# Three small moves in a graph network with expert layers: gate spread, one residual sum, first tile's norm

## The chip, the cores and the metric

The kernel runs on one core of a Trainium2 chip. Its time is the time on the device in microseconds (us), median of a few runs. Five engines work side by side, each through its own list in order: TensorE (PE in the profile, its weight loads PEld), VectorE (DVE), ScalarE (ACT), GpSimd (POOL) and SyncE (SP), which here issues the loads. They wait for each other by semaphores.

## The reference

The reference takes 625 nodes with 768 features and a list of edges and computes eight layers, always a graph layer and then an expert layer, each on the normed x and added to it (a residual). What matters here:

- Layer 0, graph attention with 12 heads of 64 features: for each head a softmax over a node's neighbours weights the neighbours' features; `out = relu(agg + res)`, where `res` is a linear map of the input. The 12 x 64 outputs side by side are added to x.
- Expert layers 0, 1 and 3: a router gives each node eight logits, the two best experts get weights from a softmax, and the output is the weighted sum of `gelu(toks @ w1e) @ w2e` over the chosen experts. An expert has 192 hidden features. In layer 1 the experts have biases, and an attention over all nodes stands before them.
- Layers 1 and 2 (graph convolutions), expert layer 2 (soft slots) and layer 3's graph attention are not touched by the change. Layer 3's graph attention needs, for every head, the products of its weights with two attention vectors; these depend on weights alone.

## The kernel before, in words

x is kept in SBUF as five tiles of 125 nodes. Instructions are written in one stream; a planner then orders them for each engine by its own estimates of time, and it may take an instruction ahead of one written before it. Tiles come from pools with a fixed number of places; in PSUM there are four places of 1024 floats, given out in the order written (`ps()`), so a new one waits until an old one has been read.

*End of layer 0* (`L0_gnn`, lines 780 to 914). For each head `gather` multiplies weights and features on PE, ACT copies the result (`gat_o`, L835), and `back` turns it back to nodes by five transposes (L848), divides by the softmax's sum and adds it to `res` on DVE (L851, L853). Two heads are one group of 128 features. After head 9 a loop (L896 to L902) takes groups 0 to 4: for groups 3 and 4 a relu on ACT (`positive`, L864), for all a sum of x and `res` on POOL (L900), then the statistics of the new x on DVE (`stats`, L868). The last head's `back` runs in two parts, tiles 0 to 3 and tile 4, and calls `last` for each tile, which adds the last group to x (L872), takes its statistics and calls `final`. `final` norms a tile (`ln_tile`, L181 to L191: mean and variance, square root on ACT, reciprocal, scaling) and turns the tile before it with `turn_due`: six transposes on PE (L198) and a copy to `xT` by ACT (L202). Both parts of the last head's `back` write one PSUM tile.

*Expert layers* (`experts`, from L962). The hidden layer has 12 blocks of 128 features, taken in pairs. A pair's products are made by a scheme of seven products of half size (`half_begin`, `half_rest`): `first` makes products 1 and 2, `rest` makes 6, 7, 5, 4 and 3, all through the helper at L136, with sums of the weights made by POOL beforehand (`sums`, L338 to L342) and sums of the results on DVE (L412, with `U2` the running one). Between the sixth and the seventh product of the first pair `choose` takes the router's logits, turns them (L260) and works out the gates on DVE (`gates`, L917 to L960). Behind the first pair, five matmuls for `gT3` (L1025) turn the gates and split them in three bf16 parts; `gate` then spreads them over 128 rows with PE (L129) and multiplies the hidden block on DVE (L1009). In expert layer 1 five more transposes (L1033) give the gates for a bias.

*Down-product* (`down`, from L1048). The first tile is multiplied as it is (60 matmuls with the first product of the next); L1080 adds it to x, and `final(0)` norms it. Then the weights' sums (`right_sums`, L444 to L447) and, for tiles 1 and 2 and then 3 and 4, seven products with sums on DVE (L1116) and one copy by ACT (L1124). The steps of layer 3's attention vectors are done beside it where there is time (`vectors`, called as `beside`): each loads 128 rows of weights through SP (L1287) into one of two places and makes two dots with them on DVE (L1298); a copy (L1297) holds them behind the work given as the second argument. In expert layers 0 and 1 seven steps are done in the down-product:

```
            prod(4, b2, (t + 1, 0))
            if t == 1:
                sums(3)
                if beside:
                    beside(7, U3[:, 0:1])
```

Of the kernel before, what the change touches and what calls it, by code (L numbers as in the profile page):

```python
# [14 lines left out]
ALU = mybir.AluOpType  # L15
# [3 lines left out]
P = 125  # L19
NT = N // P  # L20
# [3 lines left out]
NEXP = 8  # L24
# [11 lines left out]
class Net:  # L36
# [559 lines left out]
    def L0_gnn(self):  # L596
        nc, tc, a, x = self.nc, self.tc, self.a, self.x
# [4 lines left out]
        with ExitStack() as ctx:  # L602
# [236 lines left out]
            def back(h, then=None):  # L839

                o = outs[h]
                p = self.ps()[:P, 0 : NT * 128].rearrange("p (t c) -> p t c", c=128)
                rden = self.small.tile([P, NT, 1], F32, tag="rden", name="rden")
                hs = slice(h * DH, (h + 1) * DH)
                for part in (range(4), range(4, NT)) if then else (range(NT),):
                    a, b = part[0], part[-1] + 1
                    for t in part:
                        nc.tensor.transpose(  # L848
                            p[:, t, 0 : DH + 1], o[:, TILES[t]], self.ident[: DH + 1, : DH + 1]
                        )  # L850
                    nc.vector.reciprocal(rden[:, a:b], p[:, a:b, DH : DH + 1])  # L851
                    for t in part:
                        nc.vector.scalar_tensor_tensor(  # L853
                            res[:, t, hs], p[:, t, 0:DH], rden[:, t], res[:, t, hs],
                            ALU.mult, ALU.add,
                        )
                        if then:
                            then(t)
                if h % 2 and h < H - 5:
                    positive(h // 2)  # L860

            def positive(g):
                hs = slice(g * 128, (g + 1) * 128)
                nc.scalar.activation(res[:, :, hs], res[:, :, hs], AF.Relu)  # L864
# [15 lines left out]
            for i in range(H + 4):  # L880
                if i < H:
                    ms[i], us[i] = self.gat_largest(tmpp, mb, a1[i], a2[i])
                if 0 <= i - 2 < H:
                    h = i - 2
                    self.gat_exp(
                        ws[h], a1[h], us[h], a1s[:, 0, :, h], pieces=1 if i < H else NT
                    )
                steps = [(back, i - 4), (gather, i - 3)]
                for f, h in steps if i < H else reversed(steps):
                    if 0 <= h < H - (f == back):  # L890
                        f(h)
                if i < H:
                    score(i)
                if i == H + 1:

                    for g in range(H // 2 - 1):  # L896
                        if g >= H // 2 - 3:
                            positive(g)
                        hs = slice(g * 128, (g + 1) * 128)
                        nc.gpsimd.tensor_tensor(x[:, :, hs], x[:, :, hs], res[:, :, hs], ALU.add)  # L900
                        for t in range(NT):
                            stats(t, g)  # L902
            back(H - 1, then=last)
# [58 lines left out]
    def experts(self, over_all, w1, w2, gelu, b1=None, b2=None, after=None, beside=None):  # L962

        nc, tc, a, x = self.nc, self.tc, self.a, self.x
        with tc.tile_pool(name="moe", bufs=1) as big, ExitStack() as up_pool:
            bc = self.column(b1, NF) if b1 else None
            if b2:
                b2t = big.tile([NEXP, D], F32, name="b2t")
                nc.sync.dma_start(b2t, a[b2])
            hg = big.tile([128, NF, N], F32, name="hg")  # L970
            gT3 = big.tile([3 * NEXP, N], BF16, name="gT3")
            gT = big.tile([NEXP, N], F32, name="gT") if b2 else None
            sel = self.sel.rearrange("p e f -> p (e f)")
            ws = [self.weight(a[w1][:, g * 512 : (g + 1) * 512], KD, 512) for g in range(3)]
            upp = up_pool.enter_context(tc.tile_pool(name="moeup", bufs=1))
            late, prods, begun = [], {}, {}
            B = self.half_nodes(upp, late=late)


            def sums(c):  # L980
                prods[c] = self.half_products(upp, B, ws[c // 4], *(
                    slice((c % 4 + o) * 128, (c % 4 + o + 1) * 128) for o in range(2)
                ))

            def first(c):

                w, js = ws[c // 4], slice(c % 4 * 128, (c % 4 + 1) * 128)
                begun[c] = self.half_begin(
                    upp, [(w[:, ks, js], b) for ks, b in zip((slice(0, 3), slice(3, 6)), B)],
                    hg[:, c, :],  # L990
                )

            def rest(c, between=None):
                if c + 2 < NF:
                    sums(c + 2)
                self.half_rest(
                    prods.pop(c), begun.pop(c), hg[:, c, :], hg[:, c + 1, :], between
                )
                for o in range(2):
                    h = self.n3(hg[:, c + o, :])  # L1000
                    nc.scalar.activation(
                        h, h, gelu, bias=bc[:, c + o : c + o + 1] if b1 else 0.0
                    )

            def gate(c):
                gv = self.nv(self.ps(), 128)
                self.mm_nodes(gv, [sel[:, c * 128 : (c + 1) * 128]], [self.n3(gT3)])
                h = self.n3(hg[:, c, :])
                nc.vector.tensor_tensor(h, h, gv, ALU.mult)  # L1009

            sums(0)
            for c in (0, 2, 4):
                first(c)
            self.turn_due(NT - 1)
            late[0]()
            turned, gb = self.logits(big), []

            def choose():
                turned()
                gb.append(self.gates(over_all))  # L1020

            rest(0, choose)
            pv = self.nv(self.ps(), 3 * NEXP)
            for t in range(NT):
                nc.tensor.matmul(  # L1025
                    pv[:, t, :], gb[0][:, t].rearrange("p e i -> p (e i)"), self.identb[:P, :P],
                    start=True, stop=True,
                )
            nc.vector.tensor_copy(self.n3(gT3), pv)
            if b2:  # L1030
                pv = self.nv(self.ps(), NEXP)
                for t in range(NT):
                    nc.tensor.transpose(pv[:, t, :], self.lg[:, t, :], self.ident[:P, :P])  # L1033
                nc.vector.tensor_copy(self.n3(gT), pv)
            for c in range(2, NF + 2, 2):
                if c < NF:
                    if c not in begun:
                        first(c)
                    rest(c)
                for o in (c - 2, c - 1):  # L1040
                    gate(o)
                if beside and c < NF:
                    beside(1, hg[:P, c + 1, 0:1])
            up_pool.close()
            with tc.tile_pool(name="moedown", bufs=1) as dp:
                self.down(dp, a[w2], hg, gT, b2t if b2 else None, after, beside)

    def down(self, pool, w2, hg, gT, b2t, after, beside):  # L1048
# [29 lines left out]
            self.mm(p[:, 512 * j : 512 * j + HD], lhs, rhs)  # L1078
        xv = halves(x[:, 0, :])
        nc.vector.tensor_tensor(xv, xv, self.hv(p, P), ALU.add)  # L1080
        if after:
            self.final(0)
        else:
            for j in range(2):
                store(0, j)

# [13 lines left out]
        for t in (1, 3):  # L1100
# [4 lines left out]
            def prod(n, to, bias=None):  # L1105
                A, B = pr[n - 1]
                lhs = [A[:, c, :] for c in range(HB)]
                rhs = [B[:, c, :] for c in range(HB)]
                if b2t is not None and bias:
                    g, j = bias  # L1110
                    lhs.append(db[:, t // 2] if g is None else gT[:, TILES[g]])
                    rhs.append(b2t[:, j * HD : (j + 1) * HD])
                self.mm(to, lhs, rhs)

            def add(out, in0, in1=None):
                nc.vector.tensor_tensor(out, out if in1 is None else in0, in0 if in1 is None else in1, ALU.add)  # L1116
# [8 lines left out]
            add(x11, U2)  # L1125
            prod(6, a2)
            add(U2, U2, a2)
            prod(7, b1)
            add(U3, U2, b1)
            add(x12, U2)  # L1130
            prod(4, b2, (t + 1, 0))
            if t == 1:
                sums(3)
                if beside:
                    beside(7, U3[:, 0:1])
            if after:
                self.turn_due(t - 1)
            add(x21, U3)
# [17 lines left out]
                continue  # L1156
            for o in (t, t + 1):
                self.final(o, hold=True)

    def experts_beside(self, *args, **kw):  # L1160

# [1141 lines left out]
```

## Time and profile before

| what | us |
|---|---|
| median of 3 runs (1931.92 to 1932.81) | 1932.52 |
| the profiled execution | 1933.47 |
| its span | 1931.8 |
| PE busy (8314 matmuls) | 1855.9 |
| DVE, POOL, ACT busy | 1134.9, 601.8, 526.2 |
| layer 0, about 0 to 231: PE busy | 186.0 |
| expert layer 0, about 231 to 392: PE busy | 154.4 of 161 |
| attention of layer 1, about 475 to 718: PE busy | 238.2 of 243 |
| expert layer 1, about 718 to 892: PE busy | 168.0 of 174 |
| expert layer 3, about 1779 to 1932: PE busy | 144.9 of 153 |

Up to about 140 us DVE, ACT and POOL share the chain with PE; behind that PE is nearly always busy, and the chain that ended last is PE for 83% of the span. In lines of the timeline the first number is the start, the second the length; then engine, line, operation, output and inputs, shapes, and how many instructions are merged; in brackets how long the engine stood idle before, and for whom. The granted clock (PEclk) is a share of full speed. Busy time of PE contains slow matmuls too, so the clock has to be read with it.

### The profile page before, as it was taken

To read this page: it belongs to the slowest core of one execution; us is meant where nothing else is said; L and a number is where in the kernel's file an instruction comes from. 1 tells how busy PE (TensorE), PEld (TensorE's weight loads), DVE (VectorE), ACT (ScalarE), POOL (GpSimd) and SP (SyncE) were. 2 spreads that over 40 slices of the span, in tenths; PEclk is the share of its full clock that TensorE was granted. 3 is DMA by queue.
4 is the path that set the end of the run, shared out by engine and by line. 5 is a ranking of instruction groups with operands and counts; after the bars stand their busy time and mean duration, and the time that the engine had idled before them with its cause. 6 is when DMAs were issued, how large, how long until landed. Compare 5 with 4: busy or idle time off the path is not lost.

```text
span 1931.8 us, 21712 instructions
## 1 busy us (share of the span) xinstructions
PE 1855.9 (96%) x8314; PEld 1274.8 (66%) x8314; DVE 1134.9 (59%) x2226; ACT 526.2 (27%) x961; POOL 601.8 (31%) x515
## 2 busy tenths in 40 slices
PE   7968899999999999999999999999999999999999
PEld 6844565555677766655556778878667888556665
DVE  8789857647566756674835464554546555145562
ACT  2379611002254532100111131322314233111200
POOL 1079624234410052343015222231035321402331
PEclk9969899999999999999999999999999999999999
DMA  2040112120300022213510211000011121020111
GB/s 68 21 142 37 36 37 66 53 80 12 103 26 25 1 96 90 71 52 115 156 65 31 76 36 63 26 25 33 1 43 35 39 71 65 1 98 25 47 35 32
DMA packets 64021, 103.16 MB, mean 53 GB/s; under 512 B 7301, under 2 KB 37223, under 8 KB 63918
## 3 DMA queue, kind: packets, MB, share of 16 engines
q1 hardware_dynamic: 63658, 101.69, 16.2%
q8 instruction: 66, 1.08, 0.2%
q14 instruction: 37, 0.30, 0.1%
q10 hardware_dynamic: 260, 0.09, 0.0%
HBM read 99.81 MB, written 1.95 MB: 53 GB/s over the span
## 4 chain that ended last, share of the span: by engine, by line
PE 83%; DVE 7%; POOL 4%; ACT 2%; issue 1%; DMA 1%; SPq 1%; ACTq 0%; DVEq 0%; POOLq 0%
PE ps L136 65%; PE ps L129 3%; POOL gat_w L560 2%; PE ps L777 2%; PE ps L1806 2%; PE ps L1461 2%; PE ps L1493 2%; PE ps L1480 1%; PE ps L198 1%; PE ps L1675 1%; PE ps L143 1%; DMA av_w<-in_L_gnn_W 1%; PE ps L715 1%; DVE gat_w L591 1%; ACT gat_w L593 1%
## 5 line engine op out<-in xcount | busy, mean ns | idle before, releaser
L338 POOL TENSOR_TENSOR S<-w 128x384 f32<-128x384 f32 x40 | 41.5, 1042 | 453.6 <-PE ps L136 354.8
L136 PE MATMUL ps<-xT,w 128*128 128x313 f32 x480 | 137.9, 431 | 0.7 <-ACT pr L1469 0.7
L136 PE MATMUL ps<-w,xT 128*125 128x384 f32 (+2 forms) x392 | 125.3, 473 | 0.0
L136 PE MATMUL ps<-T,w 128*128 128x313 f32 x408 | 121.5, 428 | 0.0
L560 POOL TENSOR_TENSOR gat_w<-gat_w,xT 125x625 f32<-125x625 f32 x60 | 86.3, 1469 | 101.0 <-DVE xT L532 94.0
L136 PEld LDWEIGHTS ps<-xT,w 128*128 128x128 f32 x480 | 89.1, 190 | 35.1 <-issue 2.7
L136 PE MATMUL ps<-T,S 128*128 128x313 f32 x348 | 107.5, 444 | 1.8 <-DVE T L318 1.4
L136 PEld LDWEIGHTS ps<-w,xT 128*125 128x125 f32 x392 | 72.8, 188 | 46.6 <-issue 11.7
L136 PE MATMUL ps<-w,S 128*125 128x384 f32 x292 | 100.2, 488 | 2.8 <-DVE x L1116 2.8
L136 PE MATMUL ps<-xT,S 128*128 128x313 f32 x336 | 102.7, 433 | 0.0
L136 PE MATMUL ps<-w,hg 128*125 128x384 f32 x288 | 96.5, 488 | 0.9 <-DVE hg L1009 0.9
L136 PEld LDWEIGHTS ps<-T,w 128*128 128x128 f32 x408 | 76.0, 189 | 29.9 <-DVE U L358 1.4
L136 PE MATMUL ps<-hh,gat_w 125*125 125x257 f32 (+1 forms) x400 | 89.8, 379 | 0.0
L136 PEld LDWEIGHTS ps<-T,S 128*128 128x128 f32 x348 | 65.6, 195 | 30.7 <-issue 5.1
L136 PE MATMUL ps<-w,x2T 128*125 128x384 f32 (+1 forms) x280 | 84.1, 449 | 0.0
L136 PEld LDWEIGHTS ps<-w,S 128*125 128x125 f32 x292 | 54.3, 188 | 43.9 <-DVE x L1116 4.0
L136 PEld LDWEIGHTS ps<-hh,gat_w 125*125 125x125 f32 x400 | 73.3, 187 | 11.3 <-issue 0.4
L136 PEld LDWEIGHTS ps<-w,hg 128*125 128x125 f32 x288 | 53.1, 188 | 39.9 <-issue 2.2
L777 PE MATMUL ps<-ohd,ohs 125*125 125x313 bf16 x425 | 66.4, 312 | 12.2 <-DVE ohs L770 12.2
L136 PEld LDWEIGHTS ps<-xT,S 128*128 128x128 f32 x336 | 61.0, 189 | 25.0 <-issue 4.1
L1298 DVE CUSTOM_DVE_ANT_0 av_junk<-av_w,av_a 128x512 f32<-128x512 f32 (+1 forms) x80 | 72.2, 902 | 8.9 <-DMA av_w<-in_L_gnn_W 7.2
L569 DVE CUSTOM_DVE_ANT_0 junk<-ps,mb 125x625 f32<-125x625 f32 x85 | 68.5, 806 | 13.5 <-PE ps L143 8.7
(442 smaller groups left out, 3795.9 us busy)
## 6 DMA issues: line engine op xcount, KB each, us to landing
w<-in_L_ffn_phiT SPq DMA_DIRECT2D x8, 1536.0 KB
w<-in_L_gnn_W SPq DMA_DIRECT2D x8, 1536.0 KB
w<-in_L_ffn_w SPq DMA_DIRECT2D x6, 1152.0 KB
w<-in_L_gnn_W SPq DMA_DIRECT2D x6, 1152.0 KB
av_w<-in_L_gnn_W SPq DMA_DIRECT2D x24, 256.0 KB
av_w<-in_L_gnn_W SPq DMA_DIRECT2D x16, 384.0 KB
w<-in_L_ffn_w SPq DMA_DIRECT2D x3, 1536.0 KB
w<-in_L_ffn_qkv_wT SPq DMA_DIRECT2D x6, 768.0 KB
```

Source lines behind the costliest of these rows:

```text
L129: self.nc.tensor.matmul(pv[:, s, :], lhs[i], rhs[i][:, s, :], start=i == 0, stop=i == n - 1)
L136: self.nc.tensor.matmul(out, lhs[i], rhs[i], start=i == 0, stop=i == n - 1)
L143: self.nc.tensor.transpose(pv[:, t, :], col(t).to_broadcast([P, rows]), self.ident[:P, :P])
L198: nc.tensor.transpose(pv[:, k, :P], src[:, k * 128 : (k + 1) * 128], self.ident[:P, :P])
L338: nc.gpsimd.tensor_tensor(S1, A21, A22, ALU.add)
L560: nc.gpsimd.tensor_tensor(w[:, s, :], w[:, s, :], lc[:, s, :], ALU.add)
L569: nc.vector.tensor_tensor_reduce(self.n3(junk), row, self.n3(mb[:, t, :]), 1.0, -3e38, ALU.subtract, ALU.max, m[:, t : t + 1],)
L777: nc.tensor.matmul(acc[j // 2][:, j % 2, :], ohs[:, TILES[j]], ohd[:, 0:HN], start=c == cs[0], stop=c == cs[-1],)
L1298: nc.vector.tensor_tensor_reduce(junk, wt, row, 1.0, 0.0, ALU.mult, ALU.add, dst)
L1461: nc.tensor.matmul(sv[r][:, s, :], qk[half[r], 0, TILES[t]], self.n3(qk[half[r], 1, :])[:, s, :], start=True, stop=True,)
L1493: nc.tensor.matmul(ov[half[r]], v[:, s, h * DH : (h + 1) * DH], pT[r][:, s, :], start=s == 0, stop=s == NT - 1,)
L1806: nc.tensor.matmul(pv[:, j, :], zTs[t][:, k, :], w2[k // 3][:, k % 3, js], start=k == 0, stop=False,)
```

## The change

1. In `back`, the second part of the last head's transposes writes a PSUM tile of its own.
2. In the loop behind head 9, group 4 (heads 8 and 9) no longer goes through a relu on ACT and a sum on POOL: one DVE step makes `max(res, 0) + x`. Group 3 stays as it was.
3. In the expert layers, the matmuls that turn the gates, and the copies of their results, become the function `chosen`, which is called between the sixth and the seventh product of the second pair (blocks 2 and 3, the third and fourth of the twelve blocks) instead of ahead of that pair.
4. In the down-product of layers with a next stage (expert layers 0 and 1), `final(0)` is called behind the sixth product of the first two tiles instead of behind the first tile, and the seven steps of attention vectors behind these tiles' norms instead of behind their fourth product.

```
@@ back @@
                     a, b = part[0], part[-1] + 1
+                    if a:
+                        p = self.ps()[:P, 0 : NT * 128].rearrange("p (t c) -> p t c", c=128)
                     for t in part:
@@ L0_gnn, the loop behind head 9 @@
                     for g in range(H // 2 - 1):
-                        if g >= H // 2 - 3:
-                            positive(g)
                         hs = slice(g * 128, (g + 1) * 128)
-                        nc.gpsimd.tensor_tensor(x[:, :, hs], x[:, :, hs], res[:, :, hs], ALU.add)
+                        if g == H // 2 - 2:
+                            nc.vector.scalar_tensor_tensor(
+                                x[:, :, hs], res[:, :, hs], 0.0, x[:, :, hs], ALU.max, ALU.add
+                            )
+                        else:
+                            if g == H // 2 - 3:
+                                positive(g)
+                            nc.gpsimd.tensor_tensor(
+                                x[:, :, hs], x[:, :, hs], res[:, :, hs], ALU.add
+                            )
                         for t in range(NT):
                             stats(t, g)
@@ experts @@
+            def chosen():
+                pv = self.nv(self.ps(), 3 * NEXP)
+                for t in range(NT):
+                    nc.tensor.matmul(
+                        pv[:, t, :], gb[0][:, t].rearrange("p e i -> p (e i)"),
+                        self.identb[:P, :P], start=True, stop=True,
+                    )
+                nc.vector.tensor_copy(self.n3(gT3), pv)
+                if b2:
...
             rest(0, choose)
-            pv = self.nv(self.ps(), 3 * NEXP)
...
             for c in range(2, NF + 2, 2):
                 if c < NF:
                     if c not in begun:
                         first(c)
-                    rest(c)
+                    rest(c, chosen if c == 2 else None)
@@ down @@
         nc.vector.tensor_tensor(xv, xv, self.hv(p, P), ALU.add)
-        if after:
-            self.final(0)
-        else:
+        if not after:
             for j in range(2):
                 store(0, j)
...
             prod(6, a2)
             add(U2, U2, a2)
+            if after and t == 1:
+                self.final(0)
             prod(7, b1)
...
             if t == 1:
                 sums(3)
-                if beside:
-                    beside(7, U3[:, 0:1])
...
             for o in (t, t + 1):
                 self.final(o, hold=True)
+            if beside and t == 1:
+                beside(7, U3[:, 0:1])
```

More of the change, by code (lines that the diff above doesn't have):

```diff
@@ L1020, in choose @@
                 gb.append(self.gates(over_all))
-            rest(0, choose)
-            pv = self.nv(self.ps(), 3 * NEXP)
[L1024 to L1034, printed above, removed]
+            def chosen():
[7 more added lines that the diff above has]
+                if b2:
+                    pv = self.nv(self.ps(), NEXP)
+                    for t in range(NT):
+                        nc.tensor.transpose(pv[:, t, :], self.lg[:, t, :], self.ident[:P, :P])
+                    nc.vector.tensor_copy(self.n3(gT), pv)
+            rest(0, choose)
             for c in range(2, NF + 2, 2):
```

## The prediction

> **What bounds the kernel now.** I read the page's slices first, then the waits of the matmul engine (PE) from 225 us on, then the chain in order of time around each wait, then the granted clock in short windows, and last the timeline of those places.
>
> ```profile
> PE   7968899999999999999999999999999999999999
> PE ps L1025 <- DVE gb L959: 7.8, 3, 2.6
> PE ps L848 <- DVE lt_r L183: 4.3, 1, 4.3
> PE ps L136 <- DVE x L1116: 2.8, 2, 1.6
> PE ps L136 <- ACT U L1124: 1.8, 2, 1.2
> ```
>
> After the first eighth of the span PE is busy in nine tenths or more of every slice, so time is won only where PE stands still or runs slowly. The waits (total, number, longest) name the few places. The change touches the first three: the spread of the gates (L1025, once in each of three expert layers), the last head of the first layer (L848), and the down-product (L1116).
>
> ```profile
> 258.97 0.45 PE ps L1025 x5
> 259.42 6.63 PE ps L136 x18
> ...
> 1801.06 4.95 PE ps L136 x18
> ```
>
> ```profile
> 258.00:260.00 2.00, 1.03 (x7) 0.88 0.00 0
> 260.00:262.00 2.00, 2.00 (x6) 0.50 0.00 0
> 262.00:264.00 2.00, 2.00 (x7) 0.77 0.00 0
> 752.00:754.00 2.00, 2.00 (x5) 0.50 0.00 0
> 1800.00:1802.00 2.00, 1.38 (x9) 1.00 0.03 8
> ```
>
> The same 18 matmuls after the gate spread take 6.63 us in the first layer and 4.95 in the last. The windows (stretch, length, PE busy, then the granted clock) say why: after the 2.6 us stall PE runs at half clock in the first two layers, not in the last. In tenths of a microsecond the half clock lasts from 259.51 to 262.92 and from 751.03 to 754.44, 3.41 us each, and costs half of that, 1.7 us.
>
> ```profile
> 222.18 1.06 DVE L868 BATCH_NORM_STATS2 st<-x 125x6 f32<-125x128 f32 x5 [2.04 <-POOL x L900]
> 224.34 0.17 DVE L851 RECIPROCAL rden<-ps 125x4 f32<-125x4 f32 x1
> 226.67 0.44 PE L848 MATMUL ps<-ident,gat_o 65*125 65x65 f32 x1 [4.28 <-DVE lt_r L183]
> 231.48 2.89 PE L198 MATMUL ps<-ident,xn 125*128 125x125 f32 x12 [1.04 <-DVE xn L191]
> 850.70 0.55 DVE L1116 TENSOR_TENSOR x<-x,ps 125x384 f32<-125x384 f32 x1
> 851.30 4.13 PE L136 MATMUL ps<-w,S 128*125 128x384 f32 x12 [1.61 <-DVE x L1116]
> ```
>
> At the end of the first layer VectorE (DVE) stands 2.04 us for POOL's last sum; the last head's division starts at 224.34 although its transposes were done at 222.40, and PE turns the last two tiles from 231.48. In the fourth layer's down-product PE stands 1.61 us for one DVE sum.
>
> **End of the first layer.** Removed: ScalarE's relu (219.82, 0.72) and POOL's sum (220.62, 1.53); added: one DVE step of 125x640 right after the statistics that end at 218.43. Its price: 0.75 to 0.80 by the L1009 row (128x625 at 1.51 for two), so about 219.2. The reciprocal of dinv waits for ScalarE until 219.9 in any case; the statistics then run 220.1 to 221.2, head 10's transposes end at 221.48, its division takes 0.18 + 1.05, and the last head's starts at 222.7 instead of 224.34: -1.6. The new PSUM tile moves the fifth tile's transposes behind the turns of tiles 0 to 2 on PE (+0.44 between two turns), and its five DVE steps (228.05 to 229.70) behind tile 2's norm, which is no longer queued after them; ScalarE now takes both square roots ahead of its copies. Stepping through: tile 0 turned from 225.9, tile 1 to 228.85, tile 2 to 230.3, the odd transposes to 230.75, tile 3 (ScalarE's norm ends 230.9) to 232.3, against 234.37. I take -2.0. Bounds: DVE beside POOL can be three times slower (L1116: 1.69 beside POOL's L466, 0.55 alone), so the new step beside POOL's five AT sums might take 2.4; that and a half clock that lasts to 235.6 as now leave -0.2. If the shorter idle (222.40 to 225.9) escapes the half clock, turns take 0.80 as at 244.37 instead of 1.45, and it is -3.4. The fifth tile's norm ends near 233.5; it is turned at 242.5, so it is covered. SP issues nothing here, and POOL's next sums (L338, from 230.00) may start 1.5 us later, when the layer's memory comes free; the first pair's end near 237 and are asked for at 245.6.
>
> [...]
>
> **Gates.** Nothing is added; five small matmuls per layer move behind the third pair's first product, 6 matmuls of 1.58 us (1792.05 to 1793.63 from start to start). Its sums by POOL were made 10 us and more before (in the first expert layer by 239.9), and its PSUM slot is the logits', long read. So it fills 1.6 of each 2.6 us gap and leaves 1.0: three times -1.6, or -4.8. Gaps of 1.0 to 1.6 us elsewhere (738, 850) show a clock of 1.00, so the half clock in two layers goes too: -1.7 (6.63 against 4.95) and -1.7: -3.4. Against it: the planner now puts the four gate products behind the fourth product, where they used to cover DVE's sums between two products. Here the three last products of the pair cover: DVE's sum after the seventh product (0.2 + 0.48) lies beside 1.1 us of the fifth. In the next pair the first attention dot (1.05 beside POOL at 272.37) is queued ahead of the U sum that PE's seventh product needs: by my steps the sum is done 10.0 to 10.6 us after the gate spread, PE asks at 10.4. I charge 0.3 for two layers (0 to 2 as bounds; the last layer has no dots). From 259 to 315 PE and its weight loads, released by PE, make the chain, so the gain reaches the end. Sum -7.9.
>
> **Down-product.** The call for the first tile's norm is written later, but in the planned order of DVE, ScalarE and PE it stands where it stood, right behind the weights' sums and ahead of ScalarE's U copy: nothing. What moves is the seven steps of attention vectors: the copy L1297 and fourteen dots now follow two sums of x, and SP's order of their loads is the same. In the fourth layer one dot that waits for its load (849.95) falls behind the sum that PE waits for: that sum can run at about 848.9, and PE's next product is ready at 849.69, so -1.6. The first dots start 0.45 later, which costs 0 to 0.45 in the second layer, where the load-paced dots stay ahead of that sum (stall 1.15). I take -1.3, bounds 0 and -1.6.
>
> **Sum.** -2.0 - 7.9 - 1.3 = -11.2 on the profiled execution's 1933.47 is 1922.3. The median of the three runs is 0.95 below that execution, where a half clock more or less could lie; subtracted from it the sum gives 1921.3. I say 1922.0. All bounds together: -13.2 from the median (1919.3) to -3.0 from the profiled time (gates -4.8 + 2, first layer -0.2, down 0; 1930.5).
>
> **Rivals.**
> - *The half clock is luck (0.12).* The two drops lie 491.52 us apart, 144 times 3.413: fixed windows. A 2.6 us gap lowers the clock only when enough of it falls in one; in the last layer it did not. If the timed runs mostly missed, there is only the idle time: -11.2 + 3.4 = -7.8, from the median 1924.7. [...]
> - *The down-product gains nothing (0.15).* Loads 0.45 later, the sum as late: 1922.0 + 1.3 = 1923.3. For: every step there is paced by loads of 3 us. Against: the order on DVE has changed just there.
> - *The gap comes back after the gates (0.08).* Dots and gate sums delay the U sum by 1.38 + 0.48 in two layers: +3.4 over what I charged, 1925.4. Against: DVE is busy some 6.6 of the pair's 12.2 us.
> - *Slower (0.07).* The fifth tile's late transposes hold DVE's queue: behind them stand its norm and T's sums (L318, 5.4 us), which the fourth group of products needs. My steps end these at 238.8; PE asks at 245.6. Up to 6.8 us late it costs nothing, at 18 the gain of 11.2 is gone, at 22 it is slower by 0.2%: about 1936.4 and up. Against: the transposes wait only for PE and a PSUM slot that is read by 222.
>
> **How the numbers follow.** Forecast 0.58, rivals 0.15, 0.12, 0.08, 0.07. The forecast, the down rival and the clock rival hold 0.85; with a margin for their own bounds I give 1919.0 to 1926.5, the forecast's own range being 1919 to 1924. 0.2%, 3.9 us, is about what a measurement can tell from no change. All but the last rival are beyond it on the fast side: 0.93; of the last, 0.03 stops within it, 0.04 is slower.
>
> **What would show it.** Right: the wait of the gate spread for DVE falls from 7.8 to about 3 us in total, 18-matmul stretches at full clock behind it, the L848 wait gone, tile turns ending near 232, the L1116 wait down to 1.2. Wrong: a new wait of a seventh product on DVE's U sum, or half clock in the windows behind the first layer beyond 235.6.

## The result and the profile after

The changed kernel takes 1917.74 us (median; 1914.33 to 1918.05) where the kernel before took 1932.66 beside it (1931.92 to 1933.35). The ratio is 0.9921, with a 95% interval of 0.9907 to 0.9934: 14.9 us faster. 1922.0 had been predicted, with a range of 1919.0 to 1926.5; the time lies 1.3 us under the range. The profiled execution of the kernel after takes 1917.89 us (span 1916.2), 15.58 less than that of before.

The waits of PE in the kernel after (total, number, longest):

```profile
PE ps L198 <- DVE lt_r L183: 3.5, 1, 3.5
PE ps L1034 <- DVE gb L968: 3.1, 3, 1.0
...
PE ps L136 <- DVE x L1125: 1.4, 1, 1.4
...
PE ps L136 <- ACT U L1133: 1.2, 1, 1.2
```

The spread of the gates (now L1034) waits 3.1 us instead of 7.8. The wait of the last head's fifth transposes is gone; in its place PE waits 3.5 us for the first normed tile. The down-products keep one wait of each kind instead of two. The chain behind the gate spread of the first expert layer (start, length, what):

```profile
255.87 0.45 PE ps L1034 x5
256.32 6.53 PE ps L136 x24
262.84 0.64 PE ps L129 x4
263.48 4.95 PE ps L136 x18
```

24 matmuls take 6.53 us, 0.27 each: full clock (1.00 granted from 255.9 to 262.8). Before, 18 took 6.63. The four gate products (L129) now run in one go of 0.64. The stretches behind the first layer (start and end, length, PE, weight loads, DVE, ACT and POOL busy, granted clock, DMA share, GB/s):

```profile
228.00:230.00 2.00, 1.92 (x10) 1.67 (x8) 0.49 (x4) 1.44 (x3) 0.00 (x0) 0.50 0.00 0
230.00:232.00 2.00, 1.64 (x7) 1.62 (x8) 1.48 (x6) 1.36 (x4) 0.24 (x1) 0.53 0.23 74
232.00:234.00 2.00, 2.00 (x9) 1.43 (x8) 1.99 (x2) 0.70 (x1) 2.00 (x2) 1.00 0.73 235
```

Half clock ends at 231.9, not at 235.6 as in the kernel before (the same view there, of PE alone):

```profile
232.00:234.00 2.00, 2.00 (x11) 0.50 0.97 347
234.00:236.00 2.00, 2.00 (x7) 0.60 0.20 76
```

The timeline of the same place:

```profile
218.09 0.81 DVE L901 SCALAR_TENSOR_TENSOR x<-res,x 125x640 f32<-125x640 f32 x1
...
222.46 0.17 DVE L853 RECIPROCAL rden<-ps 125x4 f32<-125x4 f32 x1
...
225.64 4.17 PE L198 MATMUL ps<-ident,xn 125*128 125x125 f32 x18 [3.50 <-DVE lt_r L183]
229.60 0.32 PE L850 MATMUL ps<-ident,gat_o 65*125 65x65 f32 x1
230.36 1.51 PE L198 MATMUL ps<-ident,xn 125*128 125x125 f32 x6 [0.44 <-ACT xn L189]
```

The new DVE step took 0.81 us; the last head's division starts at 222.46 instead of 224.34. Three tiles (18 matmuls) are turned without a break, and the fifth transposes come behind them.

Where the 15.58 us went, by how much sooner the same PE instruction starts in the two profiled executions:

| stretch | predicted | trace |
|---|---|---|
| up to the last head | 0 | -0.25 |
| from there to the turn of the fifth tile (244.37, now 241.27) | -2.0 | -2.85 |
| gates, first expert layer (to the down-product) | -3.15 | -3.82 |
| gates, second expert layer | -3.15 | -3.78 |
| gates, last expert layer | -1.6 | -1.87 |
| down-product, first expert layer | +0.3 | -0.41 |
| down-product, second expert layer | -1.6 | -1.87 |
| elsewhere, 1330 to 1690 us | 0 | -0.76 |

All that was predicted to shrink shrank, each part by 0.3 to 0.9 us more. The last line has nothing to do with the change: one DVE step in layer 3's graph attention started 0.4 us behind a POOL step in the execution of before, and just ahead of it in that of after.

```profile
1504.97 1.74 DVE L1983 TENSOR_SCALAR zm<-z 125x512 f32<-125x512 f32 x1
```

```profile
1492.01 0.43 DVE L1994 TENSOR_SCALAR zm<-z 125x512 f32<-125x512 f32 x1
```

The first line is of the kernel before, the second the same step after. It is a chance of single executions: in a later execution of the kernel after, PE's wait behind this step (0.6 us before) is there again with 0.8 us.

### The profile page after: what moved, and what is told of

Read it like the earlier page. It is cut to its first block, busy times and chain, and to the rows that moved or that the text cites. A ratio compares the mean times of both kernels' runs of the same rounds, so it can differ in the third digit from the quotient of the medians.

```text
span 1916.2 us, 21703 instructions
## 1 busy us (share of the span) xinstructions
PE 1849.2 (97%) x8314; PEld 1273.0 (66%) x8314; DVE 1129.8 (59%) x2227; ACT 526.0 (27%) x960; POOL 601.8 (31%) x514
## 4 chain that ended last, share of the span: by engine, by line
PE 86%; DVE 7%; POOL 3%; ACT 2%; issue 1%; DMA 1%; ACTq 0%; DVEq 0%; POOLq 0%; SPq 0%
PE ps L136 66%; PE ps L129 4%; PE ps L777 3%; POOL gat_w L560 2%; PE ps L1817 2%; PE ps L1472 2%; PE ps L1504 2%; PE ps L1491 1%; PE ps L198 1%; PE ps L1686 1%; PE ps L143 1%; PE ps L715 1%; DVE gat_w L591 1%; ACT xT L205 0%; PE ps L2002 0%
## 5 line engine op out<-in xcount | busy, mean ns | idle before, releaser
L129 PE MATMUL ps<-gat_w,ft 125*65 125x500 f32 (+1 forms) x240 | 70.5, 450 | 4.5 <-DVE gat_w L591 3.0
```

Of the source, the lines that this page charges most:

```text
L129: self.nc.tensor.matmul(pv[:, s, :], lhs[i], rhs[i][:, s, :], start=i == 0, stop=i == n - 1)
```

## The experiments

Times below are medians; "faster" is against the median of the kernel before on the same chip in the same sitting (1933.9 for the first four kernels, 1934.0 for the next four, 1932.63 for the last four), and the interval is the 95% interval of the ratio, in us.

**The parts one by one.** Three kernels each take a part of the diff into the kernel before: `gates` has `chosen` behind the sixth product, `first` the own PSUM tile and the one DVE step, `down` the later norm and dots.

> The kernel before with part 3 of the change alone (the gates turned behind the sixth product). By the prediction's terms (three gaps shortened by 1.6 us, two half clocks of 1.7 us gone, 0.3 us given back): 7.9 us faster. By the trace after (the interval from the gate spread to the down-product shortened by 3.82 us in the first expert layer, 3.78 in the second and 1.87 in the last): 9.5 us faster. If the half clock is luck and the runs before mostly missed it: 4.5 to 5 us faster.

> The kernel before with parts 1 and 2 alone (own PSUM tile for the last head's second part, one DVE step for heads 8 and 9). The prediction: 2.0 us faster. The trace after (tile 4 turned 2.85 us earlier than the clock luck ahead of it explains, and half clock for two windows of 3.41 us instead of three): 2.9 us. If the third half-clock window comes back in some runs: 1 to 2 us in the median. If these steps are covered by something later: 0.

> The kernel before with part 4 alone (norm and dots later in the down-products). The prediction: 1.3 us faster, all of it (1.6) in the second expert layer and 0.3 lost in the first. The trace after: 1.87 in the second and 0.41 won in the first, so 2.3 us. If it does nothing: 0.

| kernel | us | faster by | interval |
|---|---|---|---|
| gates | 1924.17 | 9.7 | 7.9 to 12.8 |
| first | 1930.82 | 3.1 | 1.7 to 5.0 |
| down | 1931.86 | 2.0 | 0.6 to 4.1 |

Together 14.8 us, as much as the whole change, so nothing suggests that the parts touch each other. Each median lies nearer to what the trace of the kernel after shows (9.5, 2.9, 2.3) than to what was predicted for the part (7.9, 2.0, 1.3); the intervals alone don't rule out the predicted values. Profiled executions are compared by stretches behind 190 us: ahead of that, where no kernel differs, they lie up to 4.7 us apart (`gates` against before).

**Idle time against clock.** Three matmuls that nobody reads, in the gap ahead of the gates:

```
             rest(0, choose)
-            pv = self.nv(self.ps(), 3 * NEXP)
+            p = self.ps()
+            for _ in range(3):
+                self.mm(p[:, 0 : self.HN], [self.ident], [self.xT[:, 0, 0 : self.HN]])
+            pv = self.nv(p, 3 * NEXP)
```

> The kernel before, and ahead of the gate spread, in the gap in which PE waits for the gates, three extra matmuls of 128x313 that nobody reads (1.58 us by the product of 1.58). The gates come no sooner, so the idle share of the gain cannot appear, only the clock's. If the half clock behind the gap costs 1.7 us in two layers: 3.4 us faster, and the 18 matmuls behind the spread take 4.95 us in all three layers. If the half clock is luck, or the gain is idle time alone: within 1 us of before.

1928.95 us, 5.0 faster (3.3 to 7.5). The gates come no sooner (14.59 us behind the turn of the fifth tile, in this kernel as in the one before), but the chain of this kernel reads, in the first expert layer,

```profile
258.66 0.45 PE ps L1028 x5
259.11 4.95 PE ps L136 x18
```

so the clock is worth what the theory says, in the median even the price of three gaps and not two (3 x 1.7 = 5.1; the interval holds both). A reason for three is in the kernel `first`, whose three gaps are those of before. Its chain in the last expert layer:

```profile
1796.30 0.45 PE ps L1034 x5
1796.74 6.63 PE ps L136 x18
```

Here the last gap lost the clock too, which it had not done in the profiled execution of before. The gap is the same 2.6 us; what differs is where the fixed windows of 3.41 us cut it. In the trace of before the granted clock changes at 225.38, 235.62, 259.51, 262.92, 751.03 and 754.44, whole numbers of 3.413 us apart (3, 7, 1, 143 and 1). The edges of the windows are known from the starts of the half-clock stretches, and so the idle time in the fuller of the two windows can be worked out for all fifteen such gaps of five profiled kernels (before, first, down, psum, vec):

| idle time in one window of 3.41 us | clock behind it |
|---|---|
| 1.42 (vec, last layer), 1.60 (psum, first), 1.70 (before, last) | full |
| 2.02, 2.13, 2.25, 2.30, 2.37, 2.52, and six of 2.60 | half, for one window |

A gap of 1.0 us (three each in gates, warm, after, after2 and hot) never lost it. For these gaps, with full products on both sides, the limit lies between 1.70 and 2.02 us. It is not a limit on idle time as such: behind the first layer of the kernel after, a window at half clock with only 0.63 us of idle time (225.00 to 228.42) was followed by another at half clock.

**The two halves of the first layer's part.** `psum` has the own PSUM tile alone, `vec` the one DVE step alone.

> The kernel before with part 1 alone: the last head's fifth transposes in a PSUM tile of their own. By the prediction's steps the last head's division is no earlier (DVE still waits for POOL's sum), and only the fifth tile's steps leave the path of tile 2: 0.4 us faster, up to 1.0. If parts 1 and 2 share the gain of the pair (3.1 us) evenly: 1.5 us. If the own tile is what moves everything: 3 us.

> The kernel before with part 2 alone: heads 8 and 9 in one DVE step. The prediction's steps: DVE no longer stands for POOL, the last head's division starts 1.6 to 1.9 us earlier, 1.6 to 1.9 us faster; with the third half-clock window gone as well, 2.5. If DVE next to POOL is slow and gives the time back: 0.

1931.2 us (2.8 faster, 0.8 to 4.3) and 1931.92 (2.1 faster, 0.6 to 4.1); both together 3.1. The timeline of `psum`:

```profile
227.38 4.17 PE L198 MATMUL ps<-ident,xn 125*128 125x125 f32 x18 [5.13 <-DVE lt_r L183]
231.34 0.32 PE L850 MATMUL ps<-ident,gat_o 65*125 65x65 f32 x1
232.10 0.86 PE L198 MATMUL ps<-ident,xn 125*128 125x125 f32 x6 [0.44 <-ACT xn L189]
```

and of `vec`:

```profile
223.53 0.44 PE L848 MATMUL ps<-ident,gat_o 65*125 65x65 f32 x1 [2.65 <-DVE lt_r L183]
224.38 2.92 PE L198 MATMUL ps<-ident,xn 125*128 125x125 f32 x12 [0.41 <-DVE lt_r L183]
228.34 2.89 PE L198 MATMUL ps<-ident,xn 125*128 125x125 f32 x12 [1.05 <-DVE xn L191]
```

From the last head's first transposes to the turn of the fifth tile it takes 22.62 us in the kernel before, 21.50 in `vec`, 20.76 in `psum` and 19.5 to 19.8 with both. So by these traces the own tile is the larger half (1.9 against 1.1), more than the 0.4 to 1.0 expected of it, although the division is no earlier with it: it takes out the break between tiles 1 and 2 (1.05 us in `vec`), and with it the third half-clock window (the 36 products behind the turns take 9.73 us, in `vec` 10.87). The medians don't tell the halves apart, and each trace is one execution: in the five kernels whose first layer is unchanged this stretch takes 22.38 to 23.56 us, so which half is larger is not certain.

**Keeping the clock there as well.** The kernel after, with six such matmuls behind the last head's first four transposes:

```
+                    if then and not a:
+                        d = self.ps()
+                        for _ in range(6):
+                            self.mm(d[:, 0 : self.HN], [self.ident], [self.xT[:, 0, 0 : self.HN]])
                     nc.vector.reciprocal(rden[:, a:b], p[:, a:b, DH : DH + 1])
```

> The kernel after, and behind the last head's first four transposes six matmuls of 128x313 that nobody reads (3.2 us at full clock), in the 3.5 us in which PE waits for the first layer's first normed tile. If the half clock behind this gap (two windows of 3.41 us, 225.1 to 231.9) comes from the gap, it goes or halves: 1.7 to 3 us faster than the kernel after, 16.6 to 18 in all. If it comes from the sparse work ahead of the gap, the extra matmuls run at half clock, last 6.3 us and hold up the turns: 12 to 14.5 in all.

1916.66 us, 17.3 faster than before (15.5 to 20.7). The windows of this kernel:

```profile
224.00:226.00 2.00, 1.41 (x9) 0.71 (x7) 1.93 (x9) 0.88 (x2) 0.00 (x0) 1.00 0.04 8
226.00:228.00 2.00, 0.86 (x6) 0.63 (x6) 0.94 (x4) 1.95 (x5) 0.00 (x0) 1.00 0.00 0
```

The half clock is gone, so it does come from the gap. But the stretch takes 19.11 us against 19.78 in the kernel after: 0.7 us (0.4 against the 19.50 of `first`, whose first layer is the same), less than the 1.7 to 3 expected of it. PE is busy 0.86 of 2 us here and waits for DVE and ACT between the turns; a faster clock only lengthens its waits (0.57, 0.99 and 0.52 us between the turns, in the kernel after one of 0.44). What the median shows beyond that is not explained by this trace, and lies within the interval.

**Gates later still.** The kernel after, with `chosen` called behind the fifth product of the second pair (blocks 2 and 3; the prediction and the expectation call it the third).

```
+        if then:
+            then()
         prod(4, b2)
...
-                    rest(c, chosen if c == 2 else None)
+                    rest(c, then=chosen if c == 2 else None)
```

> The kernel after with the gates turned still later, behind the third pair's fifth product (two products more of 1.58 us). The gap that is left in the kernel after (1.03, 1.01 and 1.03 us) closes: 14.9 + 3.1 = 18.0 us faster than the kernel before. If the gates are then late for their own products, PE waits at the first gate product for the copy of the turned gates instead: 14.9, and a wait for gT3 shows.

1917.53 us, 16.5 faster (14.5 to 19.7). The wait of the gate spread is gone, and another has come, once in each expert layer (this kernel's waits, and the timeline of DVE in the first):

```profile
PE ps L136 <- DVE U L412: 2.5, 3, 0.9
```

```profile
254.79 0.92 DVE L970 CAST gb<-gr 125x40 bf16<-125x40 f32 x1
255.61 0.47 DVE L412 TENSOR_TENSOR hg<-hg,ps 128x313 f32<-128x313 f32 x1
256.00 0.47 DVE L412 TENSOR_TENSOR U<-U,ps 128x313 f32<-128x313 f32 x1
```

PE's seventh product goes into the PSUM tile that the U sum reads, so it waits for that sum, and the sum is queued on DVE behind the same chain that makes the gates. In the first layer the first gate product starts 21.45 us behind the turn of the fifth tile, against 21.50 in the kernel after: nothing is won. It is neither of the two waits expected. It is the end of the gates' chain on DVE that comes late, wherever the gates are then used.

**What makes the gates late.** The end of that chain in the kernel before, with POOL beside it:

```profile
254.69 0.21 DVE L955 CAST gb<-lg 125x40 bf16<-125x40 f32 x1
...
255.98 1.04 DVE L957 CAST gb<-gr 125x40 bf16<-125x40 f32 x1
257.05 0.92 DVE L958 TENSOR_TENSOR gr<-gr,gb 125x40 f32<-125x40 f32 x1
258.00 0.92 DVE L959 CAST gb<-gr 125x40 bf16<-125x40 f32 x1
...
255.97 0.99 POOL L339 TENSOR_TENSOR S<-S,w 128x384 f32<-128x384 f32 x1
256.92 0.99 POOL L341 TENSOR_TENSOR w<-w 128x384 f32<-128x384 f32 x1
257.87 0.99 POOL L342 TENSOR_TENSOR S<-w,S 128x384 f32<-128x384 f32 x1
```

A cast of 125x40 takes 0.21 us at 254.69, and 1.04 and 0.92 from 255.98 on: each of the last three DVE steps ends 0.06 us behind the end of a POOL sum. In `quiet_b` POOL's four sums wait for the gates by one copied element (the product that reads them starts 11 us behind them); `quiet_a` is the same in the kernel after, `best` the same with the six matmuls of `hot`.

```
     def half_products(self, pool, B, w, j0, j1, behind=None):
...
+        if behind is not None:
+            nc.gpsimd.tensor_copy(S1[:P, 0, 0:1], behind[:, NT - 1, NEXP - 1, 2:3])
         nc.gpsimd.tensor_tensor(S1, A21, A22, ALU.add)
...
             prods[c] = self.half_products(upp, B, ws[c // 4], *(
...
-                ))
+                ), behind=gb[0] if c == 4 else None)
```

> The kernel before, and POOL's four sums for the third pair held back by one copied element until the gates are made. Theory: the gates are late because four small DVE steps (125x40) run one for one beside these four POOL sums, 0.65, 1.05, 0.93 and 0.93 us where the like steps ahead of them take 0.20. Without POOL beside them they take 0.8 in all, the gates are ready 2.7 us sooner, and the wait of 2.6 us falls under 0.3 in each expert layer, with the half clock behind it: 7.8 us of idle and 3.4 to 5.1 of half clock, 11 to 13 us faster. Rival: these steps are slow by their shape (two-byte elements with a stride of three), not by POOL: within 1 us of before.

> The kernel after, with the same hold. Theory: the last 1.0 us of each gap closes and DVE's U sum, which is queued behind the gates, comes sooner as well: 3.1 us faster than the kernel after, 18.0 than before. Rival: as in the kernel with the gates behind the fifth product another wait takes its place (POOL's sums, now 2.5 us later, for the third pair): 14.9 to 16.5.

> The kernel after, with the hold of POOL's sums and with the six extra matmuls ahead of the first layer's turns. If both gains add up: 3.1 + 0.7 to 1.5, that is 18.7 to 19.5 us faster than the kernel before. If the clock behind the first layer is lost again elsewhere: 18.0.

> The kernel after once more, on the same chip and next to the same runs of the kernel before as the three others, so that differences of 1 us can be read: 14.9 us faster than before.

| kernel | us | faster by | interval |
|---|---|---|---|
| quiet_b | 1920.67 | 12.0 | 9.9 to 14.7 |
| quiet_a | 1914.41 | 18.2 | 15.3 to 21.1 |
| best | 1913.73 | 18.9 | 16.6 to 21.8 |
| after2 (the kernel after) | 1917.13 | 15.5 | 13.3 to 18.6 |

The same steps in `quiet_b`:

```profile
253.76 0.19 DVE L958 TENSOR_TENSOR gr<-lg,gb 125x40 f32<-125x40 f32 x1
253.99 0.20 DVE L959 CAST gb<-gr 125x40 bf16<-125x40 f32 x1
254.23 0.20 DVE L960 TENSOR_TENSOR gr<-gr,gb 125x40 f32<-125x40 f32 x1
254.46 0.20 DVE L961 CAST gb<-gr 125x40 bf16<-125x40 f32 x1
```

0.2 us each, by the same instructions on the same shapes: it was POOL, and not the stride. The gate spread waits for nothing in any of the three layers, and one held-back POOL step wins 12.0 us in the kernel before, where moving the gates won 9.7 (the two intervals overlap). In the kernel after it closes the rest of the gaps (2.7 us faster than `after2`). `best` is 3.4 us faster than `after2`; the 0.7 between it and `quiet_a` is less than these medians can tell apart, and the stretch behind the first layer agrees with 0.4 of it (19.10 us against 19.50).

## Why the prediction was wrong where it was

The places, the mechanisms and the sign of nearly every term were right, and the sum of 11.2 us was 3.7 too small against the medians (14.9). By the medians of the parts, 1.8 us of it lie in the gates, 1.1 at the end of the first layer and 0.7 in the down-product. The terms that were mis-sized:

- **End of the first layer: "I take -2.0".** The new DVE step (0.75 to 0.80 forecast, 0.81 measured), the division's start (-1.6 forecast, -1.88), and the end of the turns "to 232.3" (231.9) came out close to the steps. The gain at the next fixed point, the turn of the fifth tile, is 2.85, and 3.1 by the medians. Up to the first product behind the turns (231.66 for 234.16, less the 0.25 that lies ahead of this stretch) the gain is 2.25, near the forecast. The other 0.6 comes in the next 1.5 us of products: one half-clock window of three falls away, and they run at full clock. The prediction had a lower bound for "half clock that lasts to 235.6" but took no gain for its end. It also gave the own PSUM tile a cost of 0.44 us "between two turns" and only a small gain (0.4 to 1.0 in the expectation for `psum`); alone it shortened the stretch by 1.9 in one execution.
- **Gates: "Against it ... I charge 0.3".** The idle term (three times 1.6) and the half-clock term (1.7 each) are in the trace as forecast. The charge has the wrong sign. In the last layer, where no half clock played a part, the gain is 1.87, 0.3 over the 1.58; from the gate spread to the down-product `gates` is faster than `warm`, from which it differs neither in clock nor in the length of the gap, by 2.13, 2.10 and 1.88 us, that is 0.55, 0.52 and 0.30 over the 1.58. The planner puts the four gate products of a pair in one place where there were two, for two pairs in the first two of these layers and for one in the last. In one go they take 0.64 us, against 0.32 and 0.42, and the f32 products around them are broken up once less: by estimate from these differences about 0.27 us for each break that is gone. No U sum came late in the kernel after; it did in `later5`, by 2.5 us in three layers.
- **"In the last layer it did not."** This was read from one execution as if it belonged to the layer. It belongs to the window: the last gap lost the clock in `first`, `down` and `psum`. By fifteen gaps the clock falls in 12, so a sum over executions should by estimate have had some 3 x 0.8 x 1.7 = 4.1 us of half clock instead of 3.4. That is the rival "half clock is luck" with the other sign: the execution shown had slightly less of it than the five have on average, not more.
- **Down-product: "-1.3".** The second expert layer gave 1.87 (1.6 forecast); the 0.27 over the wait is not accounted for. For the first "0 to +0.45" was wrong: it gains 0.41. The wait for the sum of x grew as feared (1.1 to 1.4 us in the kernels without part 4, 1.4 to 1.6 in those with it), but the second pair's wait for ScalarE's copy of U (0.6 us) is gone in every profiled kernel with part 4 and there in every one without it. Its waits in `down`, first expert layer:

```profile
PE ps L136 <- DVE x L1114: 1.5, 1, 1.5
PE ps L136 <- ACT U L1122: 1.2, 1, 1.2
```

The norms' square roots stand ahead of that copy on ScalarE. Here they are in `down`, and then in the kernel before:

```profile
364.26 0.48 ACT L182 ACTIVATE lt_r<-lt_mv,eps 125x1 f32<-125x1 f32 x2 [18.44 <-DVE lt_mv L181]
```

```profile
367.26 0.48 ACT L182 ACTIVATE lt_r<-lt_mv,eps 125x1 f32<-125x1 f32 x2 [20.31 <-DVE lt_mv L181]
367.64 0.46 ACT L1124 COPY U<-ps 125x384 f32<-125x384 f32 x1
```

They start 3.0 us sooner, and the stage itself 1.1 us sooner (337.00 for 338.12): 1.9 us sooner within the stage. The prediction found ScalarE's planned order unchanged and did not step through when its copy would run.

Of the rivals, "the down-product gains nothing" and "the gap comes back" did not happen, and the fifth tile's late transposes hold nothing up: behind them the fifth tile is turned 3.10 us sooner, and the gate spread follows it by the same 14.60 us. The bound of 2.4 us for the new DVE step beside POOL was not reached: it took 0.81 us, and it was POOL that paid (its first AT sum, beside the step, takes 1.19 us in the kernel after, 0.45 in the kernel before). But what the L1116 row shows, a DVE step three times slower beside POOL (1.69 us for 0.55), was not carried on to the one place where it decides: there it makes the gap at the gates. The row for it was in the timeline of before (0.92 to 1.04 us for steps of 0.21).

## What to carry to other kernels

When a short chain on VectorE ends a wait of PE, look at what GpSimd does beside it before moving the consumer: a few large sums of GpSimd that nobody needed soon made the small steps here up to five times as long (1.04 us for 0.20), and holding them back won at least as much here (12.0 us) as rearranging the products (9.7). Price a PE stall not only by its length but by the half clock behind it (1.7 us for a window here), and take the chance of that from several executions, since it depended here on where the windows fell (12 of 15 gaps). Count the breaks between products of different kinds, and follow every queue that a moved step leaves, the ones that seem unconcerned too.

## What the runs showed of the hardware

- The clock was lowered by windows that were partly, not wholly, idle: at the gates 2.02 us of idle time in a window of 3.41 us did it, 1.70 did not. At half clock 0.63 us was followed by half clock again (the kernel after, 225.00 to 228.42), so idle time alone does not decide, and what else counts stays open. The windows are fixed in the trace of before: its two drops at the gates lie 491.52 us apart, 144 windows of 3.413.
- Matmuls whose result nobody reads kept the clock up: three of them in the gap of 2.6 us made the kernel 5.0 us faster without making anything earlier (the 18 matmuls behind the spread take 4.95 us for 6.63). Where PE waits for other engines between its steps, as behind the first layer, the clock kept so was worth much less (0.4 to 0.7 us for 6.83 us of half clock).
- VectorE's small steps at the end of the gates' chain (125x40) ran one for one with GpSimd's sums: 0.65 to 1.05 us each, 0.19 to 0.20 with GpSimd silent. This holds for the casts with one input as well as for the sums with two; the sums that read PSUM (L412) keep their 0.47 to 0.48 beside GpSimd (254.82 and 271.97 in the kernel before). GpSimd paid in turn: beside the new step of 0.81 us an AT sum takes 1.19 us instead of 0.45.
